# Last batch of layer 0: first softmax's exps and transposes in later steps; last batch of layer 1: relu of p4's halves on VectorE

## The chip, the cores and the metric

The kernel runs on one core of a Trainium2 chip. The metric is the device time of one execution in microseconds (us): the median of three runs.

## The reference

Two graph layers on x of 16 batches x 1024 nodes x 512 features, all in fp32, with one 1024 x 1024 matrix adj for all batches. Cut to what is computed:

```python
# layer 0
h = jnp.maximum(_layernorm(x, axis=-1), 0.0)
x = x + (einsum('nm,bmd->bnd', adj, h) @ weight + bias)
# layer 1
h = jnp.maximum(_layernorm(x, axis=-1), 0.0)
hw = einsum('bnc,cf->bnf', h, W)
s1, s2 = hw @ a[:F, 0], hw @ a[F:, 0]
e = leaky_relu(s1[:, :, None] + s2[:, None, :], 0.2) * adj[None]
att = softmax(e, axis=2)
x = x + elu(einsum('bij,bjf->bif', att, hw) + beta * hw)
```

## The kernel before, in words

The 1024 nodes are split in 128-row tiles, and every large product (adj with h, the result with the weight, and in layer 1 the same with the softmax in adj's place) is done by a seven-product scheme on halves: products p1 to p7 (`PRODUCTS`, line 48) in place of eight, paid with sums and differences of blocks on VectorE. The seven products of adj with h in layer 0, and p4 of layer 1, are split a second time in the same way: seven inner steps r1 to r7 (`inner_steps`, line 197; in layer 0 from the second batch on), each two matmul calls with 256 columns, which the profile shows as four rows of 128 x 256.

**Two loops over 16 batches.** Layer 0 runs for all batches, then layer 1 for all batches. Of each, a first part ("a") does the products with adj or with the softmax, a second ("b", class `Weighted`) those with the weight. For layer 0's batches after the first, part a is `products_a2` (line 300): the products in pairs p1/p2, p6/p5, p7/p3, whose inner steps alternate on TensorE, and then p4, whose inner steps alternate with the first weighted steps (`with_weighted`, line 259). Each product's two inner results (`y` and `x`) share one PSUM bank; ACT copies some of them out (`t[:, 0]`, `t5`, `t[:, 2]`), VectorE adds the others. In p4 the order is r1 r2 r5 r4 r6 r3 r7; after r6 VectorE makes `t[:, 1]` out of y, and r7 adds to y only after that (names in the profile: y_p4y, y_p4t).

**The order around it is written out by hand.** Every engine runs its instructions in program order (class `InOrder`, line 111). After each step k, the function `after(k)` issues what a table of plans lists for k. In `products_a2` k counts 0 to 27: seven steps for each pair of products (two inner steps of TensorE per k), then seven for p4. `plan_out` (line 1151) lists what the batch before still needs (norm, relu, logits, stores, loads), and for the last batch, 15, the tables `FIRST_A` (line 1221) and, in part b, `FIRST_B` add the softmax of batch 0 for layer 1. Their names, for a tile g of 128 x 1024 logits:
- `Rg`, `reload` (line 773): SP loads the masked logits of tile g back from DRAM, 512 KB, into a buffer of the pool `b4` (12 buffers, shared with inner sums, block results and sums); in the profile er<-ed.
- `Eg`, `exp` (line 825): four exps of 128 x 256 on ACT with their row sums (er<-er,nm).
- `Vg`, `turn` (line 836): two 128 x 512 transposes on VectorE out of the exps (pT<-er); the buffer is free after it.
- `B`, `b` only name buffers; `S` spreads the row sums of tiles 0 to 3 through DRAM, `D` puts the diagonal in. `T1a` and the like are sums of softmax blocks.

A load waits on SP for a free buffer, and all that is queued behind it on SP waits with it. Within one k the entries of `plan_out` come first, then `FIRST_A`, then loads of layer 1's operand (k = 22 and 25).

**Layer 1's end.** In layer 1 each product of the weighted part ends in `done`, which calls `elu` (line 918): `parts` reads the result z of a half (two groups of 128 x 256, g scaled by the softmax's 1/sum, `sc`) and makes relu(z) in r and exp(z) in ez, all on ACT; `total` adds r to the residual and then min(ez, 1), on VectorE, and `store` writes the rows with four transfers, for the lower nodes of the last batch two from SP and two from ACT. For the last batch (`end`) total and store of a half are issued at the next k, so those of p4's first half come after p4's second half has been through `parts`. The order of products is `NODES_LAST`: p1 p5 p2 p6 p3 p7 p4. p4's result (nh = 1, oh = 0) is read by `parts` out of its PSUM bank; p7's and p3's lie in SBUF by then. After the last batch nothing follows.

All instructions carry line 119 in the profile (the helper of `InOrder`), so groups are told apart by their tiles.

Of the kernel before, what the change touches and what calls it, by code (L numbers as in the profile page):

```python
# [30 lines left out]
AF = mybir.ActivationFunctionType  # L31
ALU = mybir.AluOpType
# [34 lines left out]
def kernel(  # L67
# [12 lines left out]
    B, N, D = x.shape  # L80
# [30 lines left out]
    class InOrder:  # L111
# [9 lines left out]
    pe, dve, act, pool, sp = (  # L121
        InOrder(e) for e in (nc.tensor, nc.vector, nc.scalar, nc.gpsimd, nc.sync)
    )

    def add(o, i0, i1, op=ALU.add):
        dve.tensor_tensor(o, i0, i1, op=op)
# [148 lines left out]
    def products_a(name, a_blk, b_blk, after, products=PRODUCTS, s4=None, p4=None):  # L275


        banks = {}

        def fork(p):  # L280
            banks["W", p] = bank(f"{name}_W{p}")
            return banks["W", p]

        read = ReadA(name, fork if products is FORKED else None, s4)
        for n, (prod, an, bn, kind, first, last) in enumerate(products):
            if prod == "p4" and p4:
                inner, weighted = p4
                inn = inner_steps(name, prod, inner(), read, banks, ld, "ld")
                with_weighted(inn, read, weighted, lambda m: None, lambda m: after(2 * n + m))
                break  # L290
            for p in range(2):
                if first:
                    banks[kind, p] = bank(f"{name}_{kind}{p}")
                ps = banks[kind, p]
                plain_a(ps, p, partial(a_blk, an), partial(b_blk, bn), range(HC), first, last)
                read(prod, p, ps)
                after(2 * n + p)
        return read.left()
# [219 lines left out]
    def node_rows(t, b):  # L518

        return [t[b, ts(s, SN), :].rearrange("(g q) d -> q g d", q=Q) for s in range(G)]  # L520
# [49 lines left out]
    def beside(plan):  # L570
        def run(k):
            for f, *args in plan.get(k, ()):
                f(*args)

        return run
# [158 lines left out]
    def u_blk(b, n, k):  # L734
        t = uts[b]
        if n in ("S1", "S2", "S4"):
            return t[n][:, k, :]
        jh = {"A11": 0, "S3": 0, "A12": 1, "A22": 1}[n]
        lo = {"A11": 0, "S3": HD, "A12": 0, "A22": HD}[n]
        return t[f"U{jh}{k // 2}"][:, k % 2, lo : lo + HD]  # L740
# [169 lines left out]
    def layer1(b, plan_a, plan):  # L910

        rs = sms[b].rs
        rows = node_rows(out, b)
        end = b == B - 1
        zs = {}
        sums = {}

        def elu(nh, oh, q, z, k):

            if end:  # L920
                r = b4.tile([P, 2, HD], F32, tag="b4", name=f"r_{b}_{nh}{oh}{q}")
            else:
                if (nh, q) not in sums:
                    sums[nh, q] = xp.tile([P, 2, D], F32, tag="xp", name=f"o_{b}_{nh}{q}")
                r = sums[nh, q][:, :, ts(oh, HD)]
            g0 = HC * nh + 2 * q
            ez = zs.pop((nh, oh, q), None)
            if ez is None:
                ez = b2.tile([P, 2, HD], F32, tag="b2", name=f"ez_{b}_{nh}{oh}{q}")

            def parts():
                for i in range(2):
                    sc = rs[:, g0 + i : g0 + i + 1]
                    act.activation(r[:, i, :], z[:, i, :], AF.Relu, scale=sc)
                    act.activation(ez[:, i, :], z[:, i, :], AF.Exp, scale=sc)

            if end or ez is not z:
                parts()
            else:
                later.setdefault(k + 1, []).append(parts)  # L940
            full = x1s[b, nh, q] if end else sums[nh, q]

            def total():
                d = full[:, :, ts(oh, HD)]
                if end:
                    add(d, d, r)
                dve.scalar_tensor_tensor(d, ez, 1.0, d, op0=ALU.min, op1=ALU.add)
                if nh != oh and not end:
                    pool.dma_start(
                        out=full.rearrange("p k d -> p (k d)"), in_=x1d[b][nh, q],  # L950
                        accum_op=ALU.add,
                    )

            def store():
                for s in range(G):
                    (act if end and nh and s % 2 else sp).dma_start(
                        out=rows[s][:, ts(2 * nh + q, 2), :], in_=full[ts(s, Q)]
                    )

            later.setdefault(k + (1 if end else 2 if ez is not z else 3), []).append(total)  # L960
            if nh != oh:
                later.setdefault(k + (1 if end else 7), []).append(store)

        products = NODES_LAST if end else P5_EARLY
        at = {p[0]: 2 * n for n, p in enumerate(products)}
        weighted1 = []

        def part(nh, oh, q, ps):
            zs[nh, oh, q] = b2.tile([P, 2, HD], F32, tag="b2", name=f"z_{b}_{nh}{oh}{q}")
            act.copy(zs[nh, oh, q], ps)  # L970

        def rest(nh, oh, q, ps, k):
            z = zs[nh, oh, q]
            add(z, ps, z)
            elu(nh, oh, q, z, k)

        def done(prod, q, ps):
            if prod == "p1":
                weighted1[0].fork("W", q, ps)
            elif prod == "p6":  # L980
                part(0, 1, q, ps)
            elif prod == "p5":
                part(1, 1, q, ps)
            elif prod == "p7":
                rest(1, 1, q, ps, at[prod] + q)
            elif prod == "p3":
                rest(0, 1, q, ps, at[prod] + q)
            else:
                elu(0 if prod == "p2" else 1, 0, q, ps, at[prod] + q)

        def after(k):
            for f in later.pop(k, ()):
                f()
            beside(plan)(k)

        weighted1.append(Weighted(f"pq{b}", w1_c, done, products))
        pT = sms[b].t

        def p4_operands():
            return partial(u_inner, b), p4_sums.pop(b), pT["T4"], p4_ext.pop(b)  # L1000

        beside(plan_a)(-1)
        left = products_a(
            f"z{b}", lambda n, k: u_blk(b, n, k), lambda n, k: pT[n][:, k, :], beside(plan_a),
            FORKED, p4=(p4_operands, weighted1[0]),
        )
        weighted1[0].rest(1, left, after)
# [174 lines left out]
    def plan_softmax(order, s):  # L1182
# [36 lines left out]
        13: {9: "N n"},  # L1219
    }  # L1220
    FIRST_A = {
        -1: "R0", 5: "E0", 8: "B V0 R1", 10: "E1", 12: "V1 R2", 17: "E2", 19: "V2 R3", 23: "E3",
        25: "b", 26: "V3 R4 R5",
    }
    FIRST_B = {
        2: "E4 S R6", 3: "V4 E5 R7", 4: "V5 E6", 5: "D V6 E7", 6: "V7 s", 7: "T1a", 8: "T1b",
# [122 lines left out]
```

## Time and profile before

| | |
|---|---|
| median of 3 runs | 2247.88 us (2247.74 to 2248.22) |
| the profiled execution, its own time | 2247.52 us |
| its span in the profile | 2245.6 us |
| granted TensorE clock, mean | 0.998 |
| busy: TensorE matmul / weight load | 2229.6 us / 1648.6 us |
| busy: VectorE / ACT / GpSimd | 1948.1 / 1551.3 / 245.0 us |
| batch 15 of layer 0, from its first matmul to layer 1's first | 1022.12 to 1091.26 us |
| last matmul's end | 2235.97 us |

A timeline line gives the start in us from the span's start, the duration, the engine, the operation, output and inputs by name with their shapes, the count, and in brackets how long the engine had been idle and what released it. A line of waits gives the engine and the tile that waited, what it waited for, and then the sum in us, the times and the longest. A group's line ends with its busy time and the mean of one in ns, and the idle time before it. Several like instructions in a row are merged in one line, and the duration is then that of all.

### The profile page before, as it was taken

How to read it: one execution, taken by the hardware profiler on the slowest of the kernel's cores; microseconds unless marked ns; L12 is line 12 of the kernel's file. 1: busy time of each engine (PE TensorE's matmuls, PEld its weight loads, DVE VectorE, ACT ScalarE, POOL GpSimd, SP SyncE). 2: the span in 40 equal slices, each digit the busy share in tenths (PEclk: the TensorE clock that was granted, in tenths of full speed). 3: DMA queues.
4: the chain of work that ended last, by engine and by line, in shares of the span. 5: the costliest groups of instructions: out<-in, count | busy, mean ns of one | idle time of the engine just before them, and what ended most of it. 6: DMA issues, size and time to landing. Idle time of an engine off the chain costs nothing.

```text
span 2245.6 us, 30403 instructions
## 1 busy us (share of the span) xinstructions
PE 2229.6 (99%) x8716; PEld 1648.6 (73%) x8716; DVE 1948.1 (87%) x4477; ACT 1551.3 (69%) x4138; POOL 245.0 (11%) x508
## 2 busy tenths in 40 slices
PE   9999999999999999999999999999999999999998
PEld 5788888888888888888666556665666556665565
DVE  7888898999898899889989988988889988898864
ACT  3776766676777677676566777767777776767743
POOL 1211111111111111111000000000000000000000
PEclk9999999999999999999999999999999999999999
DMA  6433454443444343345545665565654655546541
GB/s 207 145 127 120 159 172 133 140 145 120 142 160 164 130 149 122 105 151 184 191 116 161 169 176 155 153 188 157 167 176 141 191 148 149 140 141 166 159 119 50
DMA packets 194295, 336.06 MB, mean 150 GB/s; under 512 B 78800, under 2 KB 86992, under 8 KB 194128
## 3 DMA queue, kind: packets, MB, share of 16 engines
q1 hardware_dynamic: 185168, 302.15, 41.2%
q0 software_dynamic: 8640, 31.46, 7.5%
q8 instruction: 68, 1.11, 0.2%
q14 instruction: 99, 0.81, 0.1%
q10 hardware_dynamic: 320, 0.52, 0.1%
HBM read 228.33 MB, written 109.91 MB: 151 GB/s over the span
## 4 chain that ended last, share of the span: by engine, by line
PE 94%; DVE 3%; DMA 1%; ACT 1%; issue 0%; SPq 0%; POOL 0%; DVEq 0%; ACTq 0%; POOLq 0%
PE z_Y L119 15%; PE pq_Y L119 9%; PE po_Y L119 9%; PE z_X L119 9%; PE y_Y L119 8%; PE pq_X L119 5%; PE po_X L119 5%; PE z_W L119 5%; PE y_X L119 4%; PE y_W L119 3%; PE pq_W L119 2%; PE z_p4y L119 2%; PE po_W L119 2%; PE y_p3y L119 2%; PE y_p7y L119 2%; PE y_p4y L119 2%
## 5 line engine op out<-in xcount | busy, mean ns | idle before, releaser
L119 ACT ACTIVATE e<-e,nm 128x256 f32<-128x256 f32 x480 | 237.0, 497 | 47.0 <-DVE nm L119 47.0
L119 DVE CUSTOM_DVE_ANT_0 e<-e,mask 128x256 f32<-128x256 f32 x512 | 199.9, 423 | 54.2 <-ACT e L119 46.9
L119 PE MATMUL z_Y<-pT,ul_U 128*128 128x512 f32 x512 | 224.9, 592 | 0.0
L119 ACT ACTIVATE e<-s2b,s1b 128x256 f32<-128x256 f32 x512 | 214.7, 500 | 0.0
L119 PE MATMUL pq_Y<-w_c,z_C 128*128 128x256 f32 x768 | 189.1, 379 | 0.0
L119 PE MATMUL po_Y<-w_c,y_C 128*128 128x256 f32 x768 | 188.3, 379 | 0.0
L119 PEld LDWEIGHTS z_Y<-pT,ul_U 128*128 128x128 f32 x512 | 97.3, 190 | 115.6 <-issue 109.5
L119 DVE CUSTOM_DVE_ANT_0 y_S<-xr,v_bc 128x512 f32<-128x512 f32 x240 | 165.3, 689 | 8.9
L119 PEld LDWEIGHTS po_Y<-w_c,y_C 128*128 128x128 f32 x768 | 146.0, 190 | 20.2 <-ACT y_C L119 0.2
L119 PEld LDWEIGHTS pq_Y<-w_c,z_C 128*128 128x128 f32 x768 | 146.0, 190 | 19.8
L119 DVE STREAM_TRANSPOSE pT<-e 128x512 f32<-128x512 f32 x240 | 150.6, 680 | 0.0
L119 ACT ACTIVATE h<-h,nb_h,r_h 128x512 f32<-128x512 f32 (+1 forms) x132 | 98.2, 792 | 60.6 <-POOL nb_h L119 60.6
L119 ACT ACTIVATE y_S<-xr 128x512 f32<-128x512 f32 x90 | 56.7, 630 | 91.2 <-DVE xr L119 90.8
L119 POOL DMA_DIRECT2D o<-x1d x60 | 52.7, 935 | 609.7 <-DVE o L119 546.9
L119 PE MATMUL pq_X<-w_c,z_S 128*128 128x256 f32 x512 | 116.1, 380 | 0.1
L119 PE MATMUL po_X<-w_c,y_S 128*128 128x256 f32 x512 | 115.7, 379 | 0.0
L119 PE MATMUL z_W<-pT,ul_U 128*128 128x512 f32 x256 | 112.5, 592 | 0.0
L119 PE MATMUL z_X<-pT,ul_S 128*128 128x512 f32 x256 | 112.5, 592 | 0.0
L119 PE MATMUL z_Y<-pT_T,ul_S 128*128 128x512 f32 x256 | 112.5, 592 | 0.0
L119 PE MATMUL z_X<-pT_T,ul_S 128*128 128x512 f32 x256 | 112.5, 592 | 0.0
L119 PEld LDWEIGHTS pq_X<-w_c,z_S 128*128 128x128 f32 x512 | 96.5, 190 | 14.7 <-DVE z_C L119 1.2
L119 PEld LDWEIGHTS po_X<-w_c,y_S 128*128 128x128 f32 x512 | 97.3, 190 | 13.2
(259 smaller groups left out, 5236.7 us busy)
## 6 DMA issues: line engine op xcount, KB each, us to landing
mask<-maskd SPq DMA_DIRECT2D x128, 512.0 KB
h<-in_x_dram SPq DMA_DIRECT2D x64, 512.0 KB
xr<-in_x_dram SPq DMA_DIRECT2D x256, 128.0 KB
x1d<-xr SPq DMA_DIRECT2D x64, 512.0 KB
ul_U<-ud_U SPq DMA_DIRECT2D x64, 512.0 KB
ud_U<-xr SPq DMA_DIRECT2D x60, 512.0 KB
o<-x1d POOLq DMA_DIRECT2D x60, 512.0 KB, 8.3
out_dram<-o SPq DMA_DIRECT2D x240, 128.0 KB
```

The costliest lines, as they stand in the source:

```text
L119: return lambda *args, **kwargs: tc.keep_in_program_order(f(*args, **kwargs))
```

## The change

Two edits. In `FIRST_A` the steps for tiles 0 to 3 of batch 0's softmax get other places; each step issues what it issued. In `parts` the relu of a half is done on VectorE, as one tensor_scalar (multiply by `sc`, then maximum with 0) out of PSUM, where the batch is the last and the half belongs to p4; its exp stays on ACT. That is four instructions, two for each half.

```diff
                     sc = rs[:, g0 + i : g0 + i + 1]
-                    act.activation(r[:, i, :], z[:, i, :], AF.Relu, scale=sc)
+                    if end and nh and not oh:
+                        dve.tensor_scalar(
+                            r[:, i, :], z[:, i, :], sc, 0.0, op0=ALU.mult, op1=ALU.max
+                        )
+                    else:
+                        act.activation(r[:, i, :], z[:, i, :], AF.Relu, scale=sc)
                     act.activation(ez[:, i, :], z[:, i, :], AF.Exp, scale=sc)
...
     FIRST_A = {
-        -1: "R0", 5: "E0", 8: "B V0 R1", 10: "E1", 12: "V1 R2", 17: "E2", 19: "V2 R3", 23: "E3",
-        25: "b", 26: "V3 R4 R5",
+        -1: "R0", 5: "E0", 8: "B", 14: "V0 R1", 17: "E1", 20: "V1 R2", 22: "E2", 23: "V2 R3",
+        25: "b E3", 26: "V3 R4 R5",
     }
```

## The prediction

> **What bounds the kernel now.** I read the page first: TensorE is the engine to follow.
>
> ```profile
> PE 2229.6 (99%) x8716; PEld 1648.6 (73%) x8716; DVE 1948.1 (87%) x4477; ACT 1551.3 (69%) x4138; POOL 245.0 (11%) x508
> ```
>
> The span is 2245.6 us, so TensorE leaves only 16 us, and the change can touch two places. First the busy time by stretch, batch 14 of layer 0 (no softmax in it) against batch 15 (with it). After the stretch come its length and the busy us of PE, PEld, DVE, ACT, POOL:
>
> ```profile
> 955.59:1022.12 66.53, 66.53 (x310) 58.48 (x309) 59.20 (x129) 47.31 (x120) 10.93 (x26) 1.00 0.39 131
> 1022.12:1091.26 69.14, 67.81 (x310) 58.07 (x309) 64.28 (x143) 41.46 (x128) 5.57 (x14) 1.00 0.57 188
> ```
>
> Batch 15 costs 69.14 - 66.53 = 2.61 us more; that is all that moving its softmax steps can win here. The waits of TensorE in that stretch:
>
> ```profile
> PE y_p4y L119 <- DVE y_p4t L119: 0.5, 1, 0.5
> PE y_X L119 <- ACT y_C L119: 0.3, 1, 0.3
> PE y_p3y L119 <- ACT y_p3t L119: 0.2, 1, 0.2
> PE y_p5y L119 <- DVE y_p5t L119: 0.2, 1, 0.2
> ```
>
> By start-to-start gaps (a turn of four matmuls takes 0.863 us, the one after a stall 0.11 more) the last three cost 1.54 us (1045 to 1054), and product p4 another 1.13 (1063 to 1070). Then the timeline of VectorE and TensorE there:
>
> ```profile
> 1040.40 1.30 DVE L119 STREAM_TRANSPOSE pT<-er 128x512 f32<-128x512 f32 x2
> ...
> 1048.07 1.30 DVE L119 STREAM_TRANSPOSE pT<-er 128x512 f32<-128x512 f32 x2
> ...
> 1058.79 0.43 DVE L119 TENSOR_TENSOR y_p7t<-y_p7t,in_p 128x256 f32<-128x256 f32 x1 [0.71 <-ACT y_p7t L119]
> ...
> 1060.45 1.29 DVE L119 STREAM_TRANSPOSE pT<-er 128x512 f32<-128x512 f32 x2
> ...
> 1068.67 0.41 DVE L119 TENSOR_TENSOR y_p4t<-y_p4y,in_p 128x256 f32<-128x256 f32 x1
> ```
>
> Look at what is missing: between 1036.39 and 1068.67 VectorE waits once, 0.71 us. The p4 stall waits for a queue that is full.
>
> Last, the tail. TensorE ends at 2235.97:
>
> ```profile
> 2235.78 0.46 ACT L119 ACTIVATE r<-pq_Y,rs 128x256 f32<-128x256 f32 x1
> 2236.14 0.46 ACT L119 ACTIVATE ez<-pq_Y,rs 128x256 f32<-128x256 f32 x1
> ...
> 2237.79 0.69 DVE L119 SCALAR_TENSOR_TENSOR x<-ez,x 128x512 f32<-128x512 f32 x1
> 2238.51 0.32 SPq L119 DMA_DIRECT2D out_dram<-x  x1
> ```
>
> ```profile
> SPq L119 <- DMA out_dram<-x: 2.8, 2, 2.5
> ```
>
> p4's first half is summed at 2237.79 + 0.69 = 2238.48. SP stores one part at 2238.51 and then waits 2.5 us for a transfer, until 2241.31; its last three stores follow, the last at 2242.2. By the trace's operands SP's second store counts on the semaphore (107) that a store of ACT, issued with the first, still holds. So the FIRST half's sum sets the end; the second half (2239.94) has 1.8 us to spare.
>
> **What the Trainium skill says.** "Perfetto Trace Analysis", Optimization Strategy: find the gaps of the limiting engine and what ends them; done above, and the page's warning that busy PE is no measure holds, since 99% still hides 2.6 us. "VectorE: DVE Perf Modes", Why PSUM operands drop a tier: an fp32 operand in PSUM runs at 1x. The trace has no tensor_scalar out of PSUM, but the adds out of PSUM of that size (row below) fit 1x. "PSUM — Partial Sum Buffer", PSUM bank collisions: VectorE and ScalarE must not even READ one bank together, and code has to keep them apart by semaphore. No such pair is in the trace; a relative is: TensorE waited 0.22 us to write one half of a bank while ACT copied the other (y_p3y above). "DMA: Bandwidth & Descriptors", Why a DMA increments its semaphore by 16: one semaphore per transfer in flight; SP's 2.5 us wait is that.
>
> **Part 1, layer 0, by steps k.** V0 and R1 move 8 to 14, E1 10 to 17, V1 and R2 12 to 20, E2 17 to 22, V2 and R3 19 to 23, E3 23 to 25; V3, R4, R5 stay at 26. Nothing is added. An E is 4 exps, 4 x 0.49 = 2.0 us of ACT; a V two transposes, 1.22 us of VectorE.
>
> What it removes: V0 and V1 leave the queue ahead of the y_p5t and y_X adds, so these come 1.2 and 1.6 us sooner (1044.1, 1047.6); TensorE wants them at 1045.4 and 1049.7: the 1.54 us go. What is late next: the queue is first in, first out, and three V's, before and after, stand ahead of p4's y_p4t add at k=25. Walking it with the same intervals: ahead of schedule, y_p6t now waits 0.73 us for ACT's copy (1044.44 to 1045.17, TensorE's own pace); V0 runs at 50.2, V1 at 61.4, p3's six adds 62.6 to 66.8, V2 66.8 to 68.0, y_p4t at 68.6. Before: 68.67. The old idle 0.71 is swapped for a new 0.73, so the seventh step of p4 starts within 0.1 us of 1069.13: **TensorE loses 1.5 us there instead of before. Sum: 0**, bounds -0.7 (the new gap is closed) to +1.0 (y_p3t grazes TensorE at 1057.5, some steps 0.2 late).
>
> ACT and the loads: R1 on SP comes behind four loads ending at about 1049.4; R6 took 3.66 us from issue (1073.03) to its exp (1076.69), so E1 can start at 1053.1, before its place. R2 has no slot of b4 until y_p7t's buffer is free (in the old run R3 waited for that, 1059.28; now about 1058.2), so E2 runs about 1062 to 1064, ahead of V2 at 66.8. R3 takes p3's buffer, about 1061.2, lands by 1065; E3 ends about 1068.3, V3 wants it at 1070.5. SP also carries four 512 KB ul loads and R4, R5 there; R5 and with it spread_sum and R6 go out 1.2 us later, E6 ends 1079.9 instead of 1078.7 and V6 wants it at 1081.65: hidden by the full VectorE, at 1 us a us if that cover is gone.
>
> **Part 2, the tail.** Four relus of 0.46 to 0.48 us leave ACT; four tensor_scalars out of PSUM come to VectorE. Price, from the group row (adds out of PSUM, same size):
>
> ```profile
> L119 DVE TENSOR_TENSOR y_p6t<-y_p6y,in_p 128x256 f32<-128x256 f32 x15 | 6.4, 424 | 4.2 <-PE y_p6y L119 4.2
> ```
>
> 0.42 to the result, 0.34 to the next start. They wait in VectorE's queue, and ahead of the first half's sum stand ALL four, since the second half's relus are issued before it. And relu and exp of a half read one bank: I take them as taking turns, 0.04 us at each handover (as ACT after DVE, 2228.13 to 2228.17).
> - First half: relu 2235.16 (VectorE free), exp 2235.78 (ACT free) to 2236.24, relu 2236.28, exp 2236.74.
> - p7's sum behind it: 2236.62, second op 0.79 later 2237.41, next start 2238.01 (old pace 0.60).
> - Second half: relu 2238.01 to 2238.43, exp to 2238.95, relu 2238.99 (next start 2239.33).
> - p4's first sum: 2239.33, 2240.12, done 2240.81; the old one 2238.48. **+2.33.** The stores follow if the shared semaphore is dealt as before: +2.3. If the bank is read by both at once: the four cost 4 x 0.34 = 1.36, of which ACT waits of VectorE (0.20 + 0.24 + 0.06) swallow 0.5: +0.9. If SP's store no longer waits: second half done 2242.20, last store 2242.66 against 2242.2: +0.5. Below nothing only with both (second half done 2240.78, last store 2241.25: -0.9). Upper end +2.6.
>
> **Sum** for the profiled execution: 2247.52 us (span 2245.64 and 1.88 around it) + 0 + 2.3 = 2249.8. The median of three runs, 2247.88, lies 0.36 above it: 2250.2.
>
> **Rivals.**
> - (B) Reads share the bank, or the stores fall otherwise: +0.5 to +0.9, 2248.6. For it: no such wait is in the trace. Against: the page's rule.
> - (C) The stalls of layer 0 really go: -1.5, with the tail above 2248.7; with B's (+0.8) 2247.2. For it: VectorE is 1.2 us early at 1044. Against: three V's still ahead of y_p4t.
> - (D) The reload chain closes, and it is slower: at k=20 to 23 V, R, E, V follow each other in five steps of 1.3 to 1.7 us. If R2 gets not y_p7t's buffer but the one that V1 frees (1062.6), E2 runs 1066.3 to 1068.3, V2 ends 1069.5, R3 then gets V2's buffer, lands 1073.2, E3 ends 1075.2, V3 waits from 1070.5: VectorE loses 4.8 us in a stretch where it idles 0.96 + 1.74 until 1107, and those two idles shift too (the mask load waits for the stores behind the last xr add). +4.8 + 2.3: 2255. It decides if R2 is issued later than about 1061. Against: before, every load took the oldest free buffer.
>
> **Chances.** Main 0.52, B 0.2, C 0.18, D 0.08, other 0.02. A measurement tells about 0.2% (4.5 us) from no change; only D reaches 2252.4. So slower 0.08, same 0.91, faster 0.01. The range 2247.6 to 2252.0 takes in B, most of C and the upper bounds of parts 1 and 2 (+1.0 and +2.6 give 2251.5).
>
> **What would show it.** Right: y_p5y, y_X and y_p3y stalls gone, the p4 stall about 2 us, p4's seventh step near 1069.1; relu and exp of one half alternating, p4's first sum done near 2240.8. Wrong: ACT waiting for er at E2 beyond 1063, that step before 1068.5, or a last store before 2243.

## The result, and the profile after

The changed kernel takes 2251.26 us (median of 22 runs, 2249.93 to 2253.19), the kernel before beside it 2247.90 (22 runs, 2247.33 to 2249.93). The ratio is 1.0015, with a 95% interval of 1.0008 to 1.0021: 3.4 us more. The interval leaves out 1, so the kernel is slower, but by less than the 0.2% that the prediction set as its bound: "the same". The prediction said 2250.2 (2247.6 to 2252.0).

The profiled execution took 2251.33 us, its span is 2249.36 us against 2245.64: +3.72. Split at TensorE's last matmul: it starts at 2237.42 instead of 2235.59, so **+1.83 us come before the tail**, where the prediction had 0, and **+1.89 in it**, where it had +2.3.

The two stretches of layer 0 in the profile after (start and end, length, busy us of PE, PEld, DVE, ACT, POOL, then the granted clock):

```profile
955.59:1022.12 66.53, 66.53 (x310) 58.49 (x309) 59.21 (x130) 47.30 (x120) 10.93 (x26) 1.00 0.39 132
1022.12:1091.26 69.14, 67.15 (x303) 58.18 (x302) 64.22 (x141) 41.61 (x128) 5.38 (x14) 0.98 0.54 182
```

See the 0.98 in the second line; it was 1.00. The second window ends where layer 0 ended before; layer 1's first matmul now starts at 1092.92 instead of 1091.26, 1.66 us later. The waits of TensorE from 1022 to 1140, after:

```profile
PE y_p4y L119 <- DVE y_p4t L119: 2.0, 1, 2.0
PE z_p4y L119 <- ACT z_p4t L119: 1.4, 1, 1.4
```

The stalls of y_p5y, y_X and y_p3y are gone, and the p4 stall has become 2.0 us, as forecast. (By start-to-start times TensorE loses 0.23 us at y_p3y at 1057.8: the graze that the prediction named among its bounds.) The second line is in layer 1, outside of the stretch that the prediction followed. Before, it read

```profile
PE z_p4y L119 <- ACT z_p4t L119: 0.9, 1, 0.9
```

VectorE and TensorE after, by the timeline (the forecast was V1 at 61.4, V2 at 66.8, y_p4t at 68.6, the seventh step at 1069.1):

```profile
1061.57 1.30 DVE L119 STREAM_TRANSPOSE pT<-er 128x512 f32<-128x512 f32 x2
1066.86 1.30 DVE L119 STREAM_TRANSPOSE pT<-er 128x512 f32<-128x512 f32 x2
1068.65 0.41 DVE L119 TENSOR_TENSOR y_p4t<-y_p4y,in_p 128x256 f32<-128x256 f32 x1
1069.12 1.76 PE L119 MATMUL y_p4y<-adjT_T,h 128*128 128x256 f32 x4 [1.99 <-DVE y_p4t L119]
```

So the queue was walked rightly, to 0.2 us. But the four matmuls in the last line take 1.76 us instead of 1.13. Microsecond by microsecond, after:

```profile
1069.00:1070.00 1.00, 0.88 (x3) 0.78 (x4) 0.86 (x3) 0.00 (x0) 0.00 (x0) 0.74 0.67 184
1070.00:1071.00 1.00, 1.00 (x4) 0.82 (x3) 1.00 (x2) 0.09 (x1) 0.00 (x0) 0.50 0.88 289
1073.00:1074.00 1.00, 1.00 (x7) 0.87 (x6) 1.00 (x2) 1.00 (x5) 0.00 (x0) 1.00 0.08 2
```

The granted clock falls to 0.50 behind the gap, and a matmul of this form starts every 0.427 us instead of 0.216: eight intervals, 1.7 us. (A gap is from here on the time from the start of one matmul to the start of the next; TensorE's idle time in it is 0.38 us less. This one is 2.37 us long.)

The tail after, by the timeline (z is p7's, pq_Y p4's):

```profile
2236.99 0.48 DVE L119 TENSOR_SCALAR r<-pq_Y,rs 128x256 f32<-128x256 f32 x1
...
2238.09 0.48 DVE L119 TENSOR_SCALAR r<-pq_Y,rs 128x256 f32<-128x256 f32 x1 [0.63 <-ACT ez L119]
2238.50 0.68 DVE L119 TENSOR_TENSOR x<-x,r 128x512 f32<-128x512 f32 x1
2238.61 0.47 ACT L119 ACTIVATE ez<-pq_Y,rs 128x256 f32<-128x256 f32 x1 [0.55 <-DVE r L119]
...
2240.33 0.47 ACT L119 ACTIVATE ez<-pq_Y,rs 128x256 f32<-128x256 f32 x1 [1.25 <-DVE r L119]
...
2241.96 0.69 DVE L119 SCALAR_TENSOR_TENSOR x<-ez,x 128x512 f32<-128x512 f32 x1
```

relu and exp of a half alternate. Take the 1.83 us off and each time lies within 0.1 us of the forecast: relu 2235.16 (forecast 2235.16), p7's sum 2236.67 (2236.62), second half's relu 2237.99 (2238.01), first sum done 2240.82 (2240.81).

### The profile page after: what moved, and what is told of

It is laid out like the page before. It is cut to its first block, busy times and chain, and to the rows that moved or that the text cites. A ratio compares the mean times of both kernels' runs of the same rounds, so it can differ in the third digit from the quotient of the medians.

```text
span 2249.4 us, 30405 instructions
## 1 busy us (share of the span) xinstructions
PE 2230.6 (99%) x8716; PEld 1650.5 (73%) x8716; DVE 1950.6 (87%) x4481; ACT 1550.6 (69%) x4134; POOL 244.8 (11%) x508
## 4 chain that ended last, share of the span: by engine, by line
PE 96%; DVE 3%; DMA 1%; ACT 0%; issue 0%; SPq 0%; POOL 0%; DVEq 0%
PE z_Y L119 16%; PE po_Y L119 10%; PE pq_Y L119 9%; PE z_X L119 9%; PE y_Y L119 9%; PE po_X L119 5%; PE pq_X L119 5%; PE z_W L119 5%; PE y_X L119 4%; PE y_W L119 3%; PE po_W L119 2%; PE pq_W L119 2%; PE y_p6y L119 2%; PE z_p4y L119 2%; PE y_p4y L119 2%; PE y_p3y L119 2%
```

## The experiments

At first I held the fallen clock for the cause of the +1.83. Twelve kernels followed. Every time is set against the runs of the kernel before on the same chip, whose medians lie between 2247.5 and 2247.9. The ratios are taken over all fast runs and lie up to 0.0003 off the quotients of the medians.

**The edits apart.** The table alone, as in the change's second hunk:

> Only the new places of the softmax steps; the relus of p4's halves stay on ACT. Theory (full VectorE queue, then a clock that falls): the four stalls of layer 0's last batch become one of about 2.0 us ahead of p4's seventh inner step, which starts at 1069.1 as before; the gap of 2.4 us between matmuls then costs a granted clock of about 0.5 for 3 to 4 us, +1.6 us, and ACT-paced p4 of layer 1 (z_p4y) another 0.3: +1.6 to +2.1 us over the kernel before, with a mean that lies lower if the clock doesn't fall in every run. Rival 1 (the forecast on record, no clock effect): 0, granted clock as before. Rival 2 (all of the +3.4 us comes from the tail): 0 and a dip without a cost.

Measured: 2249.17 (before 2247.50), ratio 1.0007 (0.9999 to 1.0015), single times from 2247.86 to 2252.19. The relus alone, as in the change's first hunk:

> Only the four relus on VectorE; the softmax steps stay where they were. Theory (relu and exp of a half take turns on one PSUM bank, the first half's sum comes behind both halves' relus): first sum of p4 done 2.3 to 2.4 us later than before, about 2240.85, the end +1.8 us, TensorE as before and its clock near 0.998. The forecast on record: +2.3. Rival 1 (reads share the bank): first sum about +0.9. Rival 2 (all of the +3.4 us comes from layer 0): 0.

Measured: 2249.59 (2247.50), 1.0010 (1.0003 to 1.0016). First sum done at 2240.30 + 0.69 = 2240.99, less 0.16 by which TensorE's last matmul is later: 2240.83, so +2.35; from that matmul to the span's end +1.9. **By the medians both edits cost, +1.7 and +2.1, together 3.8 where the whole change has 3.4**; the table's interval still takes in 1. The tail's rival (reads share the bank) has fallen. But the table's profile doesn't fit the theory: a gap of 2.12 us ahead of the seventh step, clock 1.00 behind it; and near 1137.6 a gap of 2.38 us, with the clock at 0.50 from 1138 to 1141.

**V2 behind the add**, to shorten the queue ahead of y_p4t (against the table alone; of each line only the entries that differ):

```diff
-        22: "E2", 23: "V2 R3", 25: "b E3", 26: "V3 R4 R5",
+        22: "E2", 25: "b V2 R3", 26: "R4", 27: "E3 R5",
...
-        2: "E4 S R6",
+        2: "V3 E4 S R6",
```

> The new places of the softmax steps alone, with V2 and its load R3 one place further on, behind the y_p4t add that p4's seventh inner step waits for (V2 in part b's step 2, R3 and R4 two and none later, E3 two later). Theory (the stall is the length of the queue ahead of that add): one V of 1.2 us less ahead of it, so the step starts near 1067.9, the gap is about 1.1 us, the granted clock does not fall, and layer 0 ends about 1.2 us before the kernel before; a part of this is given back at p4 of layer 1's first batch, whose copies come at ACT's and VectorE's pace: in sum -1.2 to 0 us against the kernel before. Rival 1 (the add waits for something else than the queue, TensorE or a buffer): the step stays at 1069.1 and the time is that of the first kernel of this call. Rival 2 (the reload chain closes when V2 is late): VectorE waits for E3 or E4 after 1070, +2 us or more.

**The gap filled**, in front of the seventh step of batch 15 (`early` is set for that batch alone), again with the table alone:

```diff
+            if m == 6 and weighted.early:
+                spare = psum_y.tile([P, 512], F32, tag="psy", name="spare")
+                for _ in range(8):
+                    pe.matmul(spare[:, 0:P], ident, ident, start=True, stop=True)
             inn[m]()
```

> As the first kernel of this call, but with 8 added matmuls of 128x128 ahead of p4's seventh inner step in layer 0's last batch; their result is read by nobody. They fill the gap while the y_p4t add is waited for. Theory (the gap as such lets the clock fall): the seventh inner step starts at 1069.1 as before and runs at the full clock, so 1.6 us less than the first kernel, i.e. 0 to +0.5 us over the kernel before. Rival 1 (the clock falls for another reason than the idle gap, or its fall costs nothing): same time as the first kernel, or later by what the added matmuls take beyond the gap (under 0.5 us).

Measured: 2250.60 for the first (1.0011, 1.0005 to 1.0018), 2250.07 for the second (1.0012, 1.0003 to 1.0020), before 2247.50. Both did in layer 0 what they were to do: with V2 late the step starts at 1068.61 after a gap of 0.88 us (0.5 us were lost ahead of it at another wait, y_p4y for ACT's in_p), with the gap filled it starts at 1069.66, when the added matmuls are through, both at clock 1.00. Yet neither is faster than the table alone. **The theory that the p4 gap and its clock are the cost has fallen**, and with V2 late neither rival as written had the reason either. It stands in the waits of VectorE from 1085 to 1138, in the run with V2 late:

```profile
DVE e L119 <- DMA mask<-maskd: 4.2, 1, 4.2
```

Before it was 1.7, after 2.3, with the table alone 2.9, with the gap filled 2.5. VectorE waits there for the mask of tile 4 of layer 1's next softmax. Before, and after:

```profile
1107.35 0.42 DVE L119 CUSTOM_DVE_ANT_0 e<-e,mask 128x256 f32<-128x256 f32 x1 [1.74 <-DMA mask<-maskd]
```

```profile
1109.54 0.42 DVE L119 CUSTOM_DVE_ANT_0 e<-e,mask 128x256 f32<-128x256 f32 x1 [2.26 <-DMA mask<-maskd]
```

From there VectorE has no wait until it gives ACT the row maxima of that softmax, and then ACT has none (from 1129.80 before, 1131.92 after) up to ACT's copy z_p4t: 1107.35 + 28.36 = 1135.71 before, 1109.54 + 28.29 = 1137.83 after, 1108.96 + 28.28 = 1137.24 with the table alone, 1109.66 + 28.29 = 1137.95 with V2 late. The inner step r5 of layer 1's first p4 waits for that copy and starts 0.4 us behind it. Before, and after:

```profile
1136.11 1.13 PE L119 MATMUL z_p4y<-ext,in 128*128 128x256 f32 x4 [0.91 <-ACT z_p4t L119]
```

```profile
1138.23 1.13 PE L119 MATMUL z_p4y<-ext,in 128*128 128x256 f32 x4 [1.36 <-ACT z_p4t L119]
```

+2.12 us, of which, by difference, 0.29 are given back on the way to the tail: this is the +1.83. Why is the mask late? SP's queue, before and after:

```profile
1067.33 0.38 SPq L119 DMA_DIRECT2D sd<-sm  x1
...
1080.76 0.32 SPq L119 DMA_DIRECT2D sd<-sm  x1
...
1088.10 1.84 SPq L119 DMA_DIRECT2D mask<-maskd  x4
1090.03 5.34 SPq L119 DMA_DIRECT2D x1d<-xr  x4
...
1099.08 4.24 SPq L119 DMA_DIRECT2D mask<-maskd  x4
```

```profile
1068.60 0.42 SPq L119 DMA_DIRECT2D sd<-sm  x1
...
1082.33 0.32 SPq L119 DMA_DIRECT2D sd<-sm  x1
...
1089.47 1.84 SPq L119 DMA_DIRECT2D mask<-maskd  x4
1091.40 4.38 SPq L119 DMA_DIRECT2D x1d<-xr  x4
...
1101.35 4.00 SPq L119 DMA_DIRECT2D mask<-maskd  x4
```

R5 now waits for the buffer that V2 frees, until 1068.19, so the first sd (S) goes out 1.3 us later; behind it R6, 1.56 later (1074.59); E6 and E7 follow; the second sd (s) waits for E7's row sums, 1.57 later; the first four mask loads stand behind that, 1.4 later, and right behind them the stores x1d. Two loads of weights then wait for first masks to land (2.5 us in sum, before not at all), but the wait that ends last ahead of the second four is, before and after, for the first of these stores to land: 1099.0 and 1101.3. So the second four, tile 4's first, go out 2.3 later. VectorE has tile 4's mask 8.2 to 8.3 us after its issue before, after, with the table alone and with V2 late.

**The loads put ahead.** To test that, in the batch's part b (`L` loads the logit vectors s1b and s2b, `L0` and `L1` the first two masks; `LOGITS_B` stays for the other batches):

```diff
     LOGITS_B = {8: "L", 9: "L0", 10: "L1", 11: "e2", 12: "e3"}
+    LOGITS_FIRST = {5: "L", 6: "L0 L1", 11: "e2", 12: "e3"}
...
-        5: "D V6 E7", 6: "V7 s", 7: "T1a", 8: "T1b",
+        5: "D V6 E7", 6: "V7", 7: "s T1a", 8: "T1b",
...
-                plan_softmax(FIRST_B, sms[0]), plan_softmax(LOGITS_B, sms[1]),
+                plan_softmax(FIRST_B, sms[0]), plan_softmax(LOGITS_FIRST, sms[1]),
```

> The new places of the softmax steps alone, and in part b of that batch the loads that layer 1 waits for put ahead on SP: the logit vectors (s1b, s2b) of batch 1 at step 5 and the first two mask loads at step 6, ahead of the second store of row sums (sd), which goes to step 7. Theory M (the late reloads hold up all that stands behind them on SP: sd, sall, s1b, s2b, mask; the mask lands late, VectorE and ACT start late on layer 1's first exps, and ACT's copy z_p4t, for which TensorE waits near 1136, is late by as much): the first mask load goes out near 1080 instead of 1089.5 to 1090.7, VectorE no longer waits for a mask longer than for ACT, z_p4t is copied near 1135.8 and the gap near 1136 is 1.4 us or less; 0 to +0.4 us over the kernel before, against +1.7 with the same table and the old order. Rival K (the granted clock after the gap of 2.1 to 2.4 us ahead of p4's seventh step in layer 0 is the cost): same time as with the old order, +1.6. Rival L (the loads aren't what VectorE waits for): z_p4t stays at 1137.2 to 1137.8 and the gap at 1.7 to 2.4.

> The kernel before with the same loads put ahead on SP (logit vectors at step 5, first two mask loads at step 6, second store of row sums at step 7), neither edit of the change. Theory M: VectorE's wait for the mask (1.7 us to 1107.35) becomes a wait for ACT's e that ends at the same time (TensorE's own pace), so z_p4t stays at 1135.7 and the gap at 1.3: 0 (-0.2 to +0.1). Rival (the mask alone sets that gap): VectorE starts up to 1.7 us earlier and the gap goes, -1.2 us.

With the new table 2247.85 (2247.50), 1.0002 (0.9993 to 1.0010); with the old one 2247.40, 1.0000 (0.9992 to 1.0008). The table's loss is gone, and the order by itself gains nothing. In the run with the new table:

```profile
1080.18 1.49 SPq L119 DMA_DIRECT2D mask<-maskd  x2
```

```profile
1106.04 0.42 DVE L119 CUSTOM_DVE_ANT_0 e<-e,mask 128x256 f32<-128x256 f32 x1 [0.60 <-ACT e L119]
```

VectorE waits for ACT now, whose e comes at TensorE's pace; z_p4t is copied at 1135.55 and the gap near 1136 is 1.29 us. Theory M holds and L has fallen. K fell with the two runs above; in this one the gap ahead of the seventh step is only 1.61 us, so by itself it would not decide on K. The edit moves the logit vectors, the masks and the second sd together; which of them counts was not tried apart. The whole change with the same order:

> The whole change (both edits) with the logit vectors and the first mask loads put ahead on SP. Theory M: of the whole change's +3.4 to +3.8 us the part of layer 0 goes but for a clock that may fall at the gap ahead of p4's seventh step: +1.8 (the tail alone gave +2.1) to +2.3, i.e. 2249.3 to 2249.8. Rival K: the loss of layer 0 stays, 2251.

Measured: 2249.57 (2247.92), 1.0009 (1.0000 to 1.0017): +1.65 where the change as it is has +3.36, and the tail's share is what is left. In its profile a gap of 2.17 us ahead of the seventh step, clock 1.00. The intervals are wider than half of these differences; what carries the verdict is that the waits went where they were to go.

**The tail's two prices.** Both relus of a half ahead of its exps (against the kernel before), and the edit for the first half only (against the change):

```diff
+                    if end and nh and not oh:
+                        dve.tensor_scalar(
+                            r[:, i, :], z[:, i, :], scs[i], 0.0, op0=ALU.mult, op1=ALU.max
+                        )
...
+                if end and nh and not oh:
+                    for i in range(2):
+                        act.activation(ez[:, i, :], z[:, i, :], AF.Exp, scale=scs[i])
```

```diff
-                    if end and nh and not oh:
+                    if end and nh and not oh and not q:
```

> Only the edit of the tail, with both relus of a p4 half issued ahead of its two exps, so that a half's bank is handed over once and not three times. Theory T (relu and exp of one bank take turns, each handover costs the other engine's whole instruction): first half's relus about 2235.2 to 2236.1, p7's sum behind them, second half's relus at once, first sum of p4 done about 2239.6 (+1.15), against +2.35 with alternating order; the end +0.6 to +1.1 over the kernel before. Rival (the four relus' own time on VectorE and their place ahead of the first sum are the cost, not the turns): first sum as with the alternating order, end +1.8 to +2.1.

> Only the edit of the tail and only for p4's first half; the second half's relus stay on ACT. Theory T: two relus and one bank's turns less ahead of the first sum: done about 2239.5 (+1.0), the second half's sum about 2241.2, the end +0.5 to +1.0 over the kernel before. Rival (the first sum isn't behind the second half's relus): +1.8 to +2.1 as with both halves.

Measured: 2248.31 (2247.50), 1.0001 (0.9993 to 1.0009), and 2248.57, 1.0004 (0.9996 to 1.0012). The first sum is done at 2238.98 + 0.69 = 2239.67, and 2238.83 + 0.69 = 2239.52; less the 0.06 and 0.05 by which TensorE's last matmul is later, +1.1 and +1.0 over 2238.48, where the edit as it is has +2.35. Theory T holds in both. Of the 2.35 us one handover in place of three for each half saves 1.2, and the second half's relus ahead of the first half's sum are 1.4 (the two shares overlap). The run with both relus first:

```profile
2237.41 0.87 DVE L119 TENSOR_SCALAR r<-pq_Y,rs 128x256 f32<-128x256 f32 x2
...
2238.31 0.84 ACT L119 ACTIVATE ez<-pq_Y,rs 128x256 f32<-128x256 f32 x2 [1.34 <-DVE r L119]
```

**A faster kernel?** The gap near 1136 is there before, too; this run takes four exps from in front of the copy that ends it, in the kernel before with the loads put ahead:

```diff
+    FIRST_EXPS = {11: "E5 V4", 12: "E6 E7 V5"}
...
-            plans.append(plan_softmax(SOFTMAX_A, sms[b + 1]))
+            plans.append(plan_softmax({**SOFTMAX_A, **({} if b else FIRST_EXPS)}, sms[b + 1]))
```

> The kernel before with the mask loads put ahead (as in the run of that name, worth nothing by itself), and in layer 1's first batch four of batch 1's exps (tile 6) issued one step later, behind ACT's copy z_p4t that TensorE waits for near 1136. Theory (that copy is late by what stands ahead of it in ACT's full queue): it is done 4 x 0.49 = 2.0 us sooner or when z_p4y is there, the gap of 1.28 us near 1136 falls to under 0.3, TensorE runs 1.1 us earlier to the end: -1.1 us (2246.4 against 2247.5). Rival (the next copy, in<-z_p4y, which stands behind the moved exps, is late in its place): gap at a later z step, 0 to -0.5.

Measured: 2247.71 (2247.92), 1.0000 (0.9991 to 1.0008): nothing. z_p4t came at 1134.17 and the gap there went, but in the waits of TensorE from 1134 to 1150 there is a new one, 7.7 us on:

```profile
PE pq_X L119 <- DVE z_C L119: 0.9, 1, 0.9
```

The rival named the wrong wait, but its kind is right: behind a full ACT stands a full VectorE. No version here beats the kernel before.

**The clock by itself.** V2's two transposes done twice (the repeat writes the same again), in the table with the loads put ahead, then three times:

```diff
-        22: "E2", 23: "V2 R3",
+        22: "E2", 23: "W2 R3",
...
         def turn(self, g, again=False):
             h, i = divmod(g, HC)
+            if again:
+                self.turn(g)
+                self.e[g] = self.held
+            self.held = self.e[g]
```

> As the run with the new places of the softmax steps and the masks put ahead (2247.85), but the two transposes of V2 are done twice (the second time the same work again), 1.2 us more of VectorE ahead of the y_p4t add: the gap ahead of p4's seventh step grows from 1.6 to some 2.8 us and the step starts near 1070.2. Theory K2 (the granted clock halves for some 4 us after a gap of over 2.2 us, whatever its cause; seen so far at gaps of 2.37, 2.38 and 3.53, not at 2.12 and less): windows at clock 0.50 for about 3.5 us behind the gap, 1.6 us on top of the 1.2, +2.8 us over that run in sum. Rival (the falls of the clock seen so far were chance and have nothing to do with the length of the gap): clock 1.00, +1.2 us.

> As the run with V2 done twice, but three times: another 1.2 us of VectorE ahead of the y_p4t add, a gap of some 3.7 us ahead of p4's seventh step. Theory K3 (a gap lets the granted clock halve in a share of the executions that grows with its length: at 2.46 us the profile showed none and 13 of 21 times lay some 1.6 us above the lowest eight): the profile shows windows at clock 0.50 behind the gap, and nearly all times lie in one cluster 2.8 us above that run's lowest, near 2251.2. Rival (the two clusters come from somewhere else, such as where the mask lands): clock 1.00 behind the gap, two clusters again, 1.2 us above those of that run (2249.6 and 2251.3).

Twice: 2250.01 (2247.92), 1.0008 (1.0001 to 1.0014). The gap was 2.46 us, the step came at 1070.49, and the profile shows clock 1.00 behind it: the sharp bound at 2.2 us has fallen. But of the 21 times eight lie from 2248.33 to 2249.23 and thirteen from 2249.70 to 2251.71. The mean granted clock of an execution averages 0.9984 over the eight and 0.9975 over the thirteen; one fall to half for 3.4 us takes 3.4 / 2 / 2250 = 0.0008 off. Three times: 2251.76 (2247.79), 1.0017 (1.0010 to 1.0024); a gap of 4.45 us, 0.7 longer than worked out, and

```profile
1072.00:1073.00 1.00, 1.00 (x3) 0.74 (x3) 0.97 (x3) 0.00 (x0) 0.00 (x0) 0.50 0.75 250
1076.00:1077.00 1.00, 1.00 (x4) 0.82 (x3) 1.00 (x3) 1.00 (x6) 0.00 (x0) 0.50 0.17 5
```

clock 0.50 from 1071 to 1077, some 2.9 us of matmul time. One time is 2249.54; nine lie from 2250.97 to 2251.81, all at a mean clock of 0.998, and eight from 2252.42 to 2253.27, at 0.996 to 0.997. So longer gaps bring the fall more often, and the slower times are those with a lower mean clock. Where the fall lay in an execution that was not profiled isn't shown.

## Why the prediction was right, and where not

1. **"TensorE loses 1.5 us there instead of before. Sum: 0"** was right in layer 0's steps up to the seventh: V's, y_p4t and the step lie where the walk put them, the three stalls went, one of 2.0 us came. Its bounds (-0.7 to +1.0) named the graze of y_p3t, which came (0.23 us), and no fall of the clock.
2. **The step that failed is "R5 and with it spread_sum and R6 go out 1.2 us later, E6 ends 1079.9 instead of 1078.7 and V6 wants it at 1081.65: hidden by the full VectorE".** The delay was right in kind (R6 1.56 later, E6 ends at 1080.24), and V6 did hide it (1081.63), but only one of those who wait for it was followed. E7's row sums, the second spread_sum, the logit vectors, the first masks and the stores x1d stand behind it in the same queue of SP, and the loads that come last in it, tile 4's mask first, have no full VectorE for a cover: the mask came 2.19 late to a VectorE that already idled 1.74 us for it. Priced at 0, it cost +2.12 in the profile, less 0.29 given back. Taking it away brought +1.67 down to +0.35.
3. **The clock cost nothing more in this profile.** It made TensorE 1.7 us late, and TensorE then waited near 1136 for z_p4t all the same. Of two delays that end at one wait the longer counts. Where the fall comes behind the gap near 1136, as in the profile of the table alone, nothing hides it; that some executions of the whole change have it there too is likely from their spread (2249.93 to 2253.19), but not shown.
4. **Part 2: "First sum 2240.81. +2.33."** Measured +2.35, by the mechanism named: the turns on one bank, and all four relus ahead of the first sum. A tensor_scalar took 0.48 us and let the next instruction start 0.40 later, where 0.42 and 0.34 were taken; the first sum came on time all the same. The Trainium skill's "PSUM — Partial Sum Buffer", PSUM bank collisions, on which the choice rested, asks for semaphores between two such readers, and the trace has them: waits of 0.55 and 0.63 us between two engines that only read one bank. What the chip would do without these waits no run shows.
5. **"The stores follow if the shared semaphore is dealt as before: +2.3"** was mis-sized by 0.4: +1.9. The condition did not hold. In both profiles SP waits for ACT's first store to land, until 2.8 us after the first sum (2238.48 to 2241.31; 2242.65 to 2245.47). Before, three of SP's four stores stood behind that wait; after, SP's second store goes out ahead of it (2243.04), on a semaphore of its own, and only two are left.
6. Sum forecast 0 + 2.3; in the profile +1.83 + 1.89. That 2251.26 lies inside 2247.6 to 2252.0 is in part luck: the range reached so far up for a graze of y_p3t of up to 1.0 and a tail of up to 2.6, and what filled it was neither, but a wait in layer 1 that the sum put at nothing. Of the rivals, B fell with the first sum's time, C with the seventh step, and D had the place (the two idles of VectorE until 1107 that shift, since the mask load waits for the stores) but the wrong way into it: E2 and V3 never waited for a reload that long, SP's queue did it from k = 26 on.

## What to carry to other kernels

When a step moves on a queue, walk that queue to its next idle consumer, not to the first one that has slack: here a 1.3 us delay passed a full engine unharmed and came out 40 us later, at a load for which an engine already waited. Several short stalls before one full queue are worth nothing if they only join into one long stall behind it. Two engines that read one PSUM bank in turns wait for each other at each change of hands (0.5 to 0.6 us each in the tail), so let each do all its reads of the bank in a row: here the first sum came 1.2 us sooner for it.

## What the runs showed of the hardware

A gap of TensorE of little more than 2 us can halve its granted clock, and whether it does depends on where it falls. The traces keep each change of the clock with its time. In every one of the fourteen, all changes lie whole multiples of 3.413 us apart, so the clock changes at the borders of windows of that length, which start elsewhere in each execution (first change 4.2 to 7.4 us after the span's start). Before the tail a fall lasted one window, behind the gap of 4.45 us two. TensorE's idle time within a window, in batch 15 of layer 0 and layer 1's first p4:

| idle in one window, us | run | clock behind it |
|---|---|---|
| 3.14 | V2 three times | 0.50 |
| 3.13 | V2 late, near 1136 | 0.50 |
| 2.01 | the table alone, near 1136 | 0.50 |
| 1.99 | the change, ahead of p4's seventh step | 0.50 |
| 1.79 | the change with the loads ahead, seventh step | 1.00 |
| 1.75 | the table alone, seventh step | 1.00 |
| 1.54 | V2 twice, seventh step | 1.00 |

So in these stretches between 1.8 and 2.0 us of idle time in one window made the difference. The gap of 2.46 us (V2 twice) is longer than the one of 2.37 that brought a fall, but a border cut its 2.08 us of idle time in 0.53 and 1.54. With the borders anywhere, such a gap would reach 1.8 to 2.0 us in one window in about half of all positions (an estimate from these figures); 13 of the 21 times of that kernel lay in the slower group. Near the kernel's start, where TensorE runs other matmuls, the bound is not the same: there the clock fell behind windows with 1.91, 1.74 and 1.56 us of idle time in three traces and not behind one with 1.83 in another.

The Trainium skill's "TensorE: Matmul & The Clock Gate", What's actually happening, has an activity window of about 3.4 us that runs freely, and the traces agree. But the page asks for a whole idle window, and here 2.0 us of 3.4 were enough.
